# Chunk products added to the context by an accumulating DMA, in a two-layer graph-attention kernel

## The chip, the cores and the metric

The kernel runs on one core of one Trainium2 chip. A core has five engines that run side by side and wait for each other through semaphores: TensorE (PE in the profile, with its weight loads as PEld), VectorE (DVE), ScalarE (ACT), GpSimd (POOL) and SyncE (SP), which here issues all DMAs. The metric is the device time of one launch in microseconds (us), lower is better; of several runs the median is taken.

## The reference

Eight batches of 2048 nodes with 256 features go through two layers. Layer 0 is attention with 4 heads of width 64, in which the keys are cut into 8 chunks of 256 and each chunk has a softmax of its own; the chunk outputs are added up. Layer 1 is a graph attention whose scores are sums of one term per row and one per column. All is in float32.

```python
# layer 0
q, k, v = x @ Wq.T + bq, x @ Wk.T + bk, x @ Wv.T + bv        # 4 heads of 64
scores = einsum('bhnd,bhjcd->bhnjc', q, kc) / sqrt(64)       # j: 8 chunks, c: 256 keys
scores = where(mask == 0, -10, clip(scores, -10, 10))
attn = softmax(scores, axis=-1)                              # within each chunk
ctx = einsum('bhnjc,bhjcd->bhnd', attn, vc)                  # sums over the chunks j
h = layernorm(x + layernorm_affine(ctx @ Wo.T + bo + x))
# layer 1
Wh = h @ W
e = leaky_relu((Wh @ a1)[:, :, None] + (Wh @ a2)[:, None, :])
attention = softmax(where(adj > 0 or i == j, e, -inf))
out = layernorm(h + elu(attention @ Wh))
```

## The kernel before

Work of layer 0 is a loop `J` over 8 batches x 4 query blocks of 512 rows x 8 chunks. A query block is called a quarter here (quarter 0 to 3 of a batch). A chunk has two halves of 128 keys, and each half is one beat, or half-step: in a beat PE makes the scores of one half chunk for four heads (L689), DVE clips and masks them in PSUM (L699), ACT takes their exponential into `e` (L702). In the two beats after a chunk is complete, PE makes its products: the sums of `e` (part 2, with a matrix of ones) and the two halves of `e` times `v` (parts 0 and 1), all at L715. ACT copies the sums to `ds` (L729) and the products to `un` (L723). From `ds` a small DMA, a reciprocal on DVE (L737) and two more DMAs through HBM make `r`, one over the sum, spread over all rows of a head. Two beats later `scaled` (L745 to L753) runs: DVE multiplies `un` by `r`, into the context `ctxT` for the first chunk (L748), in place for the others (L750), and GpSimd adds the result to `ctxT` (L751), 7 times a block and 224 times in all. `ctxT` has one buffer for a block, `un` and `ds` have two.

The last addition of a block is issued at the end of one beat; the output projection `po` of that block (L331, 16 matmuls on PE, in the generator `fin`) stands at the end of the beat after. `fin` also loads x, adds the biases on GpSimd (L322, L323), makes two layer norms and stores h to HBM (`h_d`) and its transpose.

Layer 1 runs beside layer 0, behind it by somewhat more than a batch, at 1.5 of its steps per beat. One step treats 128 columns of a block of 512 rows: ACT (L524) and DVE (L528) make the leaky relu, DVE masks it (L533), ACT takes the exponential (L537), GpSimd adds it to the row sums `acc` (L546), PE multiplies with Wh (L556, in the last batch L571). A prelude per batch finds row maxima on DVE (L432). When a block of 16 steps is done, its tail `fin1` (L469 to L492) runs one piece per beat: the load of h into `hr`; division by the sum and the exponential `ex` of elu (L484); the minimum and maximum on DVE (L486) with the addition of `hr` on GpSimd (L487); the statistics of the layer norm (`st_c`, L292 to L295); normalization and the store. `hx`, `hr` and `ex` have one buffer each.

The order of the instructions on each engine is the order in which this program issues them (the schedule is written out by hand): at the end of a beat come the layer-1 products, then the pieces of the preludes, then of `fin` and `fin1` in the order in which they were begun, then the agenda, which holds `inverse`, `spread` and `scaled`. Each engine takes its instructions strictly in that order, and so does SP's queue of DMAs.

The lines that the change touches are L226, L469 to L492, L708, L728 and L751.

Of the kernel before, what the change touches and what calls it, by code (L numbers as in the profile page):

```python
# [9 lines left out]
F32 = mybir.dt.float32  # L10
# [4 lines left out]
ALU = mybir.AluOpType  # L15
# [4 lines left out]
P = 128  # L20
# [8 lines left out]
def tile_adj_attention__then__gat(  # L29
# [35 lines left out]
    nc = tc.nc  # L65
    B, N, F = x.shape
# [4 lines left out]
    IB = 512  # L71
# [151 lines left out]
    nc.sync.dma_start(out=W_aug[:, :, 0:F], in_=W.rearrange("(k p) o -> p k o", p=P))  # L223
    a_bc = []
    for n in range(2):
        t = one.tile([P, F], F32, tag=("hx", "ex")[n], name=f"a_bc{n}")  # L226
        nc.sync.dma_start(out=t, in_=a[n * F : (n + 1) * F, :].rearrange("f o -> (f o)").partition_broadcast(P))
        a_bc.append(t)

# [238 lines left out]

    def fin1(b, ib, hx, acc):  # L469

        hr = one.tile([P, TPB, F], F32, tag="hr", name=f"hr{b}_{ib}")
        nc.sync.dma_start(out=hr, in_=h_d[b, ib])
        yield


        if acc is not None:
            pr = ps_m.tile([P, TPB], F32, tag="m", name=f"pr{b}_{ib}")
            for t in range(TPB):
                nc.tensor.matmul(pr[:, t : t + 1], acc[:, ts(t, P)], ones[:, 0:1], start=True, stop=True)
            r = two.tile([P, TPB], F32, tag="r1", name=f"r1{b}_{ib}")  # L480
            nc.vector.reciprocal(r, pr)
            divided(hx, [hx[:, t, :] for t in range(TPB)], r)
        ex = one.tile([P, TPB, F], F32, tag="ex", name=f"ex{b}_{ib}")
        nc.scalar.activation(ex, hx, AF.Exp, bias=shifts[:, 2:3])  # L484
        yield
        nc.vector.scalar_tensor_tensor(hx, ex, 1.0, hx, ALU.min, ALU.max)  # L486
        nc.gpsimd.tensor_add(hx, hx, hr)  # L487
        yield
        mv, rstd = stats(hx, f"c{b}_{ib}")
        yield  # L490
        normalize(hx, mv, rstd, f"c{b}_{ib}")
        nc.sync.dma_start(out=out[b, ts(ib, IB), :].rearrange("(t p) f -> p t f", p=P), in_=hx)  # L492
# [170 lines left out]
    for J in range(total + 1):  # L663
        b, ib, j = J // (NIB * NCH), J // NCH % NIB, J % NCH
        live = J < total
        if live and j == 0:
            ctxT = one.tile([P, 2, IB], F32, tag="ctx", name=f"ctxT{b}_{ib}")
        cur = {"b": b, "ib": ib, "j": j, "es": [], "ctxT": ctxT, "v": None, "name": f"{b}_{ib}_{j}"}
        for half in range(2):
            c = 2 * j + half  # L670
            if live:

                if c % HT == 0:
                    if b == 0:
                        mk = blocks0[ib, c // HT]
                    else:
                        mk = mk0.pop((b, ib, c // HT))
                if c % HT == 1:
                    n = (b * NIB + ib) * 2 + c // HT + 1
                    nb, nib, nhf = n // (2 * NIB), n // 2 % NIB, n % 2  # L680
                    if 0 < nb < B:
                        mk0[nb, nib, nhf] = mask_block(0, nib, nhf, f"{nb}_{nib}_{nhf}")
            begin_beat(RATE if b < B - 1 else LAST_RATE)
            if live:
                scs = []
                for hp in range(NPAIR):
                    sc = ps_s.tile([P, 2, IB], F32, tag="sc", name=f"sc{b}_{ib}_{c}_{hp}")
                    for h in range(2):
                        nc.tensor.matmul(  # L689
                            sc[:, h, :],  # L690
                            kT[h * D : (h + 1) * D, hp, ts(c, P)],
                            qT[h * D : (h + 1) * D, hp, :],
                            start=True,
                            stop=True,
                        )
                    scs.append(sc)
                cap = mk[:, c % HT, :].unsqueeze(1).to_broadcast([P, 2, IB])
                for hp in range(NPAIR):
                    nc.vector.scalar_tensor_tensor(scs[hp], scs[hp], -CLIP, cap, ALU.max, ALU.min)  # L699
                for hp in range(NPAIR):  # L700
                    e = eight.tile([P, 2, IB], F32, tag="e", name=f"e{b}_{ib}_{c}_{hp}")
                    nc.scalar.activation(e, scs[hp], AF.Exp)  # L702
                    cur["es"].append(e)
            middle_of_beat()

            if prev is not None:
                if half == 0:
                    prev["un"] = two.tile([P, 2, IB], F32, tag="un", name=f"un{prev['name']}")  # L708
                for part in ((2, 0), (1,))[half]:
                    m = ps_m.tile([P, IB], F32, tag="m", name=f"u{prev['name']}_{part}")  # L710
                    for i in range(2):
                        pc = 2 * prev["j"] + i
                        for h in range(H):
                            f0 = h * D + part * DH
                            nc.tensor.matmul(  # L715
                                m[h * DH : (h + 1) * DH, :],
                                prev["v"][:, pc, f0 : f0 + DH] if part < 2 else ones[:, 0:DH],
                                prev["es"][2 * i + h // 2][:, h % 2, :],
                                start=(i == 0),
                                stop=(i == 1),  # L720
                            )
                    if part < 2:
                        nc.scalar.copy(prev["un"][:, part, :], m)  # L723
                    else:

                        ds = two.tile([P, IB], F32, tag="ds", name=f"ds{prev['name']}")  # L728
                        nc.scalar.copy(ds, m)  # L729
                        dc = two.tile([P, IB // DH], F32, tag="dc", name=f"dc{prev['name']}")  # L730
                        nc.sync.dma_start(
                            out=dc, in_=ds.rearrange("(h m) (n w) -> h m n w", m=DH, n=DH)[:, 0, :, :]
                        )
                        prev["dc"] = dc

                        def inverse(p=prev):
                            nc.vector.reciprocal(p["dc"], p["dc"])  # L737
                            p["rd"] = dram3.tile([H, IB], F32, tag="rd", name=f"rd{p['name']}")
                            nc.sync.dma_start(out=p["rd"].rearrange("h (m w) -> (h m) w", m=DH), in_=p["dc"])

                        def spread(p=prev):
                            p["r"] = two.tile([P, IB], F32, tag="r", name=f"r{p['name']}")
                            nc.sync.dma_start(out=p["r"], in_=p["rd"].unsqueeze(1).to_broadcast([H, DH, IB]))

                        def scaled(p=prev):  # L745
                            r2 = p["r"].unsqueeze(1).to_broadcast([P, 2, IB])
                            if p["j"] == 0:
                                nc.vector.tensor_mul(p["ctxT"], p["un"], r2)  # L748
                            else:
                                nc.vector.tensor_mul(p["un"], p["un"], r2)  # L750
                                nc.gpsimd.tensor_add(p["ctxT"], p["ctxT"], p["un"])  # L751
                            if p["j"] == NCH - 3:
                                fins.append(fin(p["b"], p["ib"], p["ctxT"]))  # L753

                        at(beat, inverse)
                        at(beat, spread)
                        at(beat + 2, scaled)

            end_beat()
            if half == 1:  # L760


                if live and j == NCH - 2 and J + 2 < total:
                    nb, nib = (b, ib + 1) if ib + 1 < NIB else (b + 1, 0)
                    xq = xT_tile(nb, nib, "q")
                    if nb != b:
                        tiles = [xT_tile(nb, i, "k") for i in range(2)]
                if live and j == NCH - 1 and J + 1 < total:
                    qT = make_qT(nb, nib, xq)
                    if nb != b:  # L770
                        kT = make_kT(nb, tiles)
                        tiles_v = [xT_tile(nb, i, "v") for i in range(3)]
                if live and J % (NIB * NCH) == 0:
                    if b == 0:
                        tiles_v = [xT_tile(0, i, "v") for i in range(3)]
                    v = make_v(b, tiles_v)
                if live:
                    cur["v"] = v
            beat += 1
        prev = cur if live else None  # L780
# [50 lines left out]
```

## Time and profile before

| | us |
|---|---|
| median of 3 runs | 4443.78 |
| lowest and highest | 4443.62, 4454.05 |
| the profiled execution, reported time | 4445.93 |
| its span, first to last instruction | 4444.1 |
| span without both layers side by side: first 600 us, last 644.1 us | 1244.1 |

The mean granted clock of TensorE was 0.976. The profile names a group of instructions by line, engine, operation and the tiles it writes and reads (`out<-in`). A wait "A <- B" is idle time of A's engine that ended when B finished. The chain of waits follows the work back from the last instruction. Tile names have their buffer numbers left out.

These are the DMAs that the changed lines are concerned with, from the page (issuing queue, count, size):

```profile
r<-rd SPq DMA_DIRECT2D x256, 256.0 KB
fb<-far SPq DMA_DIRECT2D x256, 256.0 KB
```

### The profile page before, as it was taken

To read this page: it belongs to the slowest core of one execution; us is meant where nothing else is said; L and a number is where in the kernel's file an instruction comes from. 1 tells how busy PE (TensorE), PEld (TensorE's weight loads), DVE (VectorE), ACT (ScalarE), POOL (GpSimd) and SP (SyncE) were. 2 spreads that over 40 slices of the span, in tenths; PEclk is the share of its full clock that TensorE was granted. 3 is DMA by queue.
4 is the path that set the end of the run, shared out by engine and by line. 5 is a ranking of instruction groups with operands and counts; after the bars stand their busy time and mean duration, and the time that the engine had idled before them with its cause. 6 is when DMAs were issued, how large, how long until landed. Compare 5 with 4: busy or idle time off the path is not lost. (4 is left out here: it accounts for less than half of the span.)

```text
span 4444.1 us, 61341 instructions
## 1 busy us (share of the span) xinstructions
PE 4076.1 (92%) x23052; PEld 1914.3 (43%) x23052; DVE 3405.3 (77%) x4527; ACT 2603.7 (59%) x3877; POOL 1776.4 (40%) x906
## 2 busy tenths in 40 slices
PE   7888999999899998999999999999989999899767
PEld 3222334444344543445334453444434444344545
DVE  4777469985799758996599866998579975898686
ACT  4665445665556655665556655666555665566445
POOL 0222224553355423554345542455325553355411
PEclk9999999999999999999999999999999999999988
DMA  4554333332322323323333223332232232332241
GB/s 149 167 164 152 92 100 101 96 93 78 105 81 91 101 64 115 89 77 92 99 99 91 78 77 104 101 101 86 84 101 87 86 103 68 118 92 73 65 136 54
DMA packets 266874, 433.98 MB, mean 98 GB/s; under 512 B 86097, under 2 KB 121169, under 8 KB 265553
## 3 DMA queue, kind: packets, MB, share of 16 engines
q1 hardware_dynamic: 266576, 430.06, 31.7%
q8 instruction: 181, 2.97, 0.3%
q14 instruction: 117, 0.95, 0.1%
HBM read 358.48 MB, written 69.40 MB: 96 GB/s over the span
## 5 line engine op out<-in xcount | busy, mean ns | idle before, releaser
L702 ACT ACTIVATE e<-sc 128x1024 f32<-128x1024 f32 x1024 | 1037.3, 1022 | 1146.7 <-DVE sc L699 1102.2
L699 DVE SCALAR_TENSOR_TENSOR sc<-sc,mk 128x1024 f32<-128x1024 f32 x1024 | 1205.8, 1222 | 512.8 <-PE sc L689 282.9
L689 PE MATMUL sc<-qT,kT 64*128 64x512 f32 x4096 | 1060.0, 632 | 106.9 <-ACT e L702 104.0
L751 POOL TENSOR_TENSOR ctxT<-ctxT,un 128x1024 f32<-128x1024 f32 x224 | 562.7, 2512 | 1164.1 <-DVE un L750 1059.1
L715 PE MATMUL u<-e,v 128*32 128x512 f32 x8192 | 980.4, 596 | 0.0
L556 PE MATMUL us<-wh,w 128*128 128x256 f32 x3584 | 875.5, 393 | 78.1 <-ACT w L537 60.5
L556 PEld LDWEIGHTS us<-wh,w 128*128 128x128 f32 x3584 | 662.8, 192 | 420.7 <-ACT w L537 117.7
L546 POOL TENSOR_TENSOR acc<-acc,w 128x512 f32<-128x512 f32 x392 | 602.7, 1537 | 541.0 <-ACT w L537 531.3
L689 PEld LDWEIGHTS sc<-qT,kT 64*128 64x128 f32 x4096 | 346.1, 188 | 627.4 <-ACT e L702 307.4
L528 DVE SCALAR_TENSOR_TENSOR w<-ab,sj,w 128x512 f32<-128x512 f32 x512 | 584.0, 1161 | 32.1 <-ACT w L524 32.1
L715 PEld LDWEIGHTS u<-e,v 128*32 128x32 f32 x8192 | 239.8, 110 | 657.7 <-issue 539.2
L533 DVE TENSOR_TENSOR w<-w,mk 128x512 f32<-128x512 f32 x512 | 475.1, 948 | 44.4 <-DMA mk<-mask 41.7
L715 PE MATMUL u<-e,ones 128*32 128x512 f32 x4096 | 498.3, 604 | 0.0
L432 DVE CUSTOM_DVE_ANT_0 fb<-sj_row,fb 128x1024 bf16<-128x1024 f32 x256 | 397.1, 1559 | 5.9 <-DMA fb<-far 5.6
L537 ACT ACTIVATE w<-w 128x512 f32<-128x512 f32 x512 | 310.7, 631 | 90.0 <-DVE w L533 89.6
L524 ACT ACTIVATE w<-ab,sj 128x512 f32<-128x512 f32 x512 | 353.3, 716 | 13.5 <-PE us L571 6.3
L750 DVE TENSOR_TENSOR un<-un,r 128x1024 f32<-128x1024 f32 x224 | 276.5, 1234 | 85.4 <-DMA r<-rd 78.8
L723 ACT COPY un<-u 128x512 f32<-128x512 f32 x512 | 300.6, 587 | 55.4 <-PE u L715 53.7
L715 PEld LDWEIGHTS u<-e,ones 128*32 128x32 f32 x4096 | 107.9, 110 | 359.5 <-issue 317.9
L737 DVE RECIPROCAL dc<-dc 128x16 f32<-128x16 f32 x256 | 64.1, 250 | 184.5 <-DMA dc<-ds 159.7
L571 PE MATMUL us<-wh,w 128*128 128x257 f32 x512 | 128.7, 413 | 45.9 <-ACT w L537 45.7
L487 POOL TENSOR_TENSOR hx<-hx,hr 128x1024 f32<-128x1024 f32 x32 | 91.6, 2862 | 191.6 <-DVE hx L486 191.6
(97 smaller groups left out, 3150.7 us busy)
## 6 DMA issues: line engine op xcount, KB each, us to landing
r<-rd SPq DMA_DIRECT2D x256, 256.0 KB
fb<-far SPq DMA_DIRECT2D x256, 256.0 KB
mk<-mask SPq DMA_DIRECT2D x120, 512.0 KB
xT_k<-in_xT_dram SPq DMA_DIRECT2D x32, 512.0 KB
raw<-in_adjT_dram SPq DMA_DIRECT2D x32, 512.0 KB
xT_q<-in_xT_dram SPq DMA_DIRECT2D x32, 512.0 KB
rawf<-in_adj_dram SPq DMA_DIRECT2D x32, 512.0 KB
xT_v<-in_xT_dram SPq DMA_DIRECT2D x32, 512.0 KB
```

The costliest lines, as they stand in the source:

```text
L432: nc.vector.tensor_tensor_reduce(out=fbs[2 * TPB * ib + n], in0=sj_row[:, ts(n % 2, HN)], in1=fbs[2 * TPB * ib + n], scale=1.0, scalar=2 * ...
L524: nc.scalar.activation(self.w, k["ab"][:, 1, :], AF.Identity, bias=k["sj"][:, 1, c : c + 1])
L528: nc.vector.scalar_tensor_tensor(self.w, k["ab"][:, 0, :], k["sj"][:, 0, c : c + 1], self.w, ALU.add, ALU.max)
L533: nc.vector.tensor_tensor(self.w, self.w, self.k["mks"][self.c // HT][:, self.c % HT, :], ALU.min)
L537: nc.scalar.activation(self.w, self.w, AF.Exp)
L546: nc.gpsimd.tensor_add(k["acc"], k["acc"], self.w)
L556: nc.tensor.matmul(k["us"][:, t, :], self.w[:, ts(t, P)], k["wh"][:, c, 0:F], start=(first and t % 2 == 0), stop=last, skip_group_check=True,)
L689: nc.tensor.matmul(sc[:, h, :], kT[h * D : (h + 1) * D, hp, ts(c, P)], qT[h * D : (h + 1) * D, hp, :], start=True, stop=True,)
L699: nc.vector.scalar_tensor_tensor(scs[hp], scs[hp], -CLIP, cap, ALU.max, ALU.min)
L702: nc.scalar.activation(e, scs[hp], AF.Exp)
L715: nc.tensor.matmul(m[h * DH : (h + 1) * DH, :], prev["v"][:, pc, f0 : f0 + DH] if part < 2 else ones[:, 0:DH], prev["es"][2 * i + h // 2][ ...
L751: nc.gpsimd.tensor_add(p["ctxT"], p["ctxT"], p["un"])
```

## The change

The product of a chunk is added to `ctxT` by a DMA from SBUF to SBUF with an add on its way, issued from GpSimd's queue, in place of GpSimd's own addition. `un` gets three buffers and `ds` one. `ex` shares the buffer of `hr` (so that h is loaded only after the minimum and maximum have read `ex`), and the addition of h moves to the beat after. A vector that is loaded once at the start, and lay in the buffer of `ex`, lies in that of `y`.

```diff
@@ a_bc @@
-        t = one.tile([P, F], F32, tag=("hx", "ex")[n], name=f"a_bc{n}")
+        t = one.tile([P, F], F32, tag=("hx", "y")[n], name=f"a_bc{n}")
@@ fin1 @@
-        hr = one.tile([P, TPB, F], F32, tag="hr", name=f"hr{b}_{ib}")
-        nc.sync.dma_start(out=hr, in_=h_d[b, ib])
         yield
...
-        ex = one.tile([P, TPB, F], F32, tag="ex", name=f"ex{b}_{ib}")
+        ex = one.tile([P, TPB, F], F32, tag="hr", name=f"ex{b}_{ib}")
         nc.scalar.activation(ex, hx, AF.Exp, bias=shifts[:, 2:3])
         yield
         nc.vector.scalar_tensor_tensor(hx, ex, 1.0, hx, ALU.min, ALU.max)
+        hr = one.tile([P, TPB, F], F32, tag="hr", name=f"hr{b}_{ib}")
+        nc.sync.dma_start(out=hr, in_=h_d[b, ib])
+        yield
         nc.gpsimd.tensor_add(hx, hx, hr)
@@ the loop over chunks @@
-                    prev["un"] = two.tile([P, 2, IB], F32, tag="un", name=f"un{prev['name']}")
+                    prev["un"] = three.tile([P, 2, IB], F32, tag="un", name=f"un{prev['name']}")
...
-                        ds = two.tile([P, IB], F32, tag="ds", name=f"ds{prev['name']}")
+                        ds = one.tile([P, IB], F32, tag="ds", name=f"ds{prev['name']}")
...
                                 nc.vector.tensor_mul(p["un"], p["un"], r2)
-                                nc.gpsimd.tensor_add(p["ctxT"], p["ctxT"], p["un"])
+                                nc.gpsimd.dma_start(out=p["ctxT"], in_=p["un"], accum_op=ALU.add)
```

## The prediction

> **What bounds the kernel now.** I read the page's first part, then busy time by stage, then the waits on TensorE, and last the timeline around single accumulations. The first line is from the page, the second from the busy times by window (columns: stretch, its length, busy us of each engine, granted clock, DMA share, GB/s).
>
> ```profile
> PE 4076.1 (92%) x23052; PEld 1914.3 (43%) x23052; DVE 3405.3 (77%) x4527; ACT 2603.7 (59%) x3877; POOL 1776.4 (40%) x906
> 600.00:3800.00 3200.00, 3044.77 (x17479) 1429.25 (x17467) 2534.46 (x3279) 1914.12 (x2881) 1417.20 (x724) 0.99 0.30 92
> ```
>
> In the 3200 us in which both layers run, PE is busy 3044.8 us, 95%. Its matmuls stand; only its 155 us of gaps there (368 us in the whole span) can shrink, and a new gap on PE is a loss almost in full. The waits view says what ends those gaps (total us, times, longest us):
>
> ```profile
> PE sc L689 <- ACT e L702: 104.0, 68, 6.6
> PE us L556 <- ACT w L537: 60.5, 49, 6.8
> PE po L331 <- POOL ctxT L751: 26.8, 16, 5.1
> ```
>
> The third is the line under change: the output projection `po` waits for the last accumulation of its block. That is 16 of 32 blocks already, so this edge has no cushion there. The add itself, and the VectorE rows that could feel it, in the groups (count | busy, mean ns | idle before):
>
> ```profile
> L751 POOL TENSOR_TENSOR ctxT<-ctxT,un 128x1024 f32<-128x1024 f32 x224 | 562.7, 2512 | 1164.1 <-DVE un L750 1059.1
> L528 DVE SCALAR_TENSOR_TENSOR w<-ab,sj,w 128x512 f32<-128x512 f32 x512 | 584.0, 1161 | 32.1 <-ACT w L524 32.1
> ```
>
> 224 adds take 562.7 us on an engine that is 40% busy, so its time as such bounds nothing. L528, whose fastest run is 649 ns and median 746, averages 1161. The timeline shows why, in one block of query quarter 3:
>
> ```profile
> 2626.64 1.22 DVE L750 TENSOR_TENSOR un<-un,r 128x1024 f32<-128x1024 f32 x1
> 2627.94 2.36 POOL L751 TENSOR_TENSOR ctxT<-ctxT,un 128x1024 f32<-128x1024 f32 x1 [3.39 <-DVE un L750]
> 2629.11 1.74 DVE L528 SCALAR_TENSOR_TENSOR w<-ab,sj,w 128x512 f32<-128x512 f32 x1
> 2636.66 3.62 PE L331 MATMUL po<-WT_o,ctxT 128*128 128x256 f32 x16
> ```
>
> L528 started beside the add and ended with it (1.74 us). Here PE came to `po` 8.80 us after L750's end (2636.66 less 2627.86), so a slow landing costs nothing. Quarter 2 is different:
>
> ```profile
> 1949.08 1.23 DVE L750 TENSOR_TENSOR un<-un,r 128x1024 f32<-128x1024 f32 x1
> 1951.16 2.34 POOL L751 TENSOR_TENSOR ctxT<-ctxT,un 128x1024 f32<-128x1024 f32 x1
> 1953.55 3.72 PE L331 MATMUL po<-WT_o,ctxT 128*128 128x256 f32 x16 [1.32 <-POOL ctxT L751]
> ```
>
> PE was free 1.93 us after L750's end and then stood still for 1.32 us.
>
> **What the Trainium skill says.** (1) "SBUF — State Buffer", Who interferes with whom: a VectorE instruction with two SBUF inputs contends with a GpSimd instruction that reads SBUF, and the second to start waits for the first. The trace agrees: over all 512 L528s, the 101 that overlap most with L751 average 1501 ns, the 180 beside no GpSimd work 736. L699, which has PSUM for one input, is 1220 ns beside L751 and 1223 alone. (2) "DMA: Bandwidth & Descriptors", Anatomy of one DMA: a DMA from GpSimd takes about 2.0 us plus bytes/436e3. No run here has such a DMA. (3) The same page, Rules for kernel authors: an accumulate reads its destination and writes it later, so a reader must wait for its semaphore; `po` then waits for landing, not for the issue. (4) "Perfetto Trace Analysis", DMA Instruction — SWDGE: the instruction's end in a profile is the end of descriptor generation, not of the movement; the POOL row will thus look short.
>
> **The change part by part.** The sum is against the profiled execution: span 4444.1, reported 4445.9 us, 2.1 above the median of 4443.8.
>
> *Landing instead of add.* Let X be the time from L750's end until `ctxT` may be read. It is now 2.4 to 3.2 us (2.49 when the add starts at once). For 512 KB formula (2) gives 3.2; the destination has to be read as well, so I count the bytes twice: an estimate of 2.0 + 2.4 = 4.4. In this trace an HBM load of the same 512 KB took 3.63 us from issue to release when quiet (chain of waits, `mk<-mask` at 4301.92) and 7.52 when crowded (at 3846.74). Behind every accumulation SP issues the 256 KB `r<-rd` within 2 us, so some crowding is regular. I take X = 5.5; bounds 4.4 and 10. From the timeline I took, for each of the 32 blocks, when PE was free for `po` after L750's end. Quarter 0: 2.58 us early to 2.3 late, mostly near 0 or 2; quarter 1: 0.0 once, else 4.7 to 5.3; quarter 2: 1.93 in six, about 0 and 3.6 in the others; quarter 3: 4.1 to 8.8. The sum of max(0, X minus that) is 53 us at 4.4, 76 at 5.5, 89 at 6, 142 at 8, 202 at 10, against today's 26.8. At 5.5: **+50 us**.
>
> *The other accumulations.* They follow each other at a median of 15.3 us, so each lands before the next; the GpSimd queue does not stall. With three `un` buffers ACT's copy L723 meets a buffer whose DMA was issued four half-steps (some 35 us) earlier, and the one `ds` buffer is refilled about 17 us after its 8 KB DMA, which takes about 2 us. All of these: 0. If X passed 15 us, POOL's sums of `w` and its layer-norm steps behind the wait would be late.
>
> *h one step later.* Instruction order on PE is the same; on DVE, ACT, POOL and SP the tail of a layer-1 block (add of h, statistics, normalization, store) moves one half-step back. In six quarter-2 blocks its statistics (nine instructions, 2.3 us, 1946.75 to 1949.1) now stand directly before L750; they go behind it, so L750 ends 2.3 us earlier against PE: 6 x 2.3 = **-14**. They then stand in the half-step with `po` and push L699 there; half of 2.3 us in six blocks reaches PE: **+7** (0 to 14). SP's h load now waits for L486 (DVE); behind it in SP's queue are `rd<-dc` and `r<-rd`, which wait for a later DVE instruction anyway, so 0. At the very end nothing covers the load. From the chain of waits (start, us, what):
>
> ```profile
> 4430.51 1.24 DVE hx L486
> 4431.86 2.34 POOL hx L487
> ```
>
> L487 follows L486 at once; a 512 KB load comes between, at the quiet 3.63: **+3.6**. The tag swap of `ex` and `a_bc` is free: nothing else holds these buffers then.
>
> *The shared port.* Without L751, 101 L528s lose about 0.77 us each and 15 L432s about 0.75 (1966 beside it, 1214 alone): 89 us of DVE. DVE is not the bound, and PE's gaps behind it (first two waits, 165 us, of which about 66 in the 3200 us) mostly follow other GpSimd adds (L322, L323). I give a quarter: **-22** (0 to -60). POOL's own 563 us shrink to descriptor writing: 0.
>
> Sum: 50 - 14 + 7 + 3.6 - 22 = +25, so 4445.9 + 24.6 = 4470.5 for such an execution, and 4468 for the median.
>
> **Rivals.** *Faster: the port decides.* Removing L751 frees VectorE not only directly; L432 and L528 pairs move up, GpSimd's remaining adds meet other instructions, and PE's 104 us of waiting for `e` melt. For it: 89 us of measured lengthening. Against it: PE is 95% busy. With X at its lower end and the port at -40: 26 - 14 + 0 + 4 - 40 = -24, 4420. It decides as soon as the port gives more than the new waiting on `po`: with X = 4.4 from 16 to 23 us of relief, with 5.5 from about 47.
> *The landing is long.* Accumulation works at less than half the copy rate, or its queue shares the engines badly; X = 8 to 10. At 8: 115 - 14 + 14 + 4 - 10 = +109, 4553; at 10 about 4610. Against it: DMA engines are only 30% busy.
> *Nothing to measure.* Relief and waiting cancel, 4440 to 4455: X near 4.8.
>
> **Chances.** Forecast (slower by up to 90 us) 0.45; long landing 0.17; faster 0.27; cancelled 0.11. About 0.3%, 13 us, is what a measurement of this kernel can tell from no change; a little of the forecast's own case falls inside it, so: faster 0.27, same 0.14, slower 0.59. The range 4420 to 4555 goes from the faster rival's worked value to the long landing at 8 us; the forecast's own is 4445 to 4515.
>
> **What would show it.** PE's wait of `po` on the DMA of `ctxT` grows from 26.8 to about 60 us, in quarters 0 and 2 most, hardly in 3; L528's mean falls from 1161 towards 1010; in the last block L487 starts some 3.6 us later after L486. I am wrong if `po` waits less than 30 us in all (X was too long), if it waits over 100 (too short), or if PE's waits for `e` and `w` fall by more than 40 us (the port was worth more).

## The result and the profile after

The change makes the kernel slower: 4597.26 us (median of 4 runs, 4590.40 to 4600.67) against 4447.48 (4 runs, 4443.62 to 4454.05); ratio 1.0343, 95% interval 1.0328 to 1.0357. That is about 150 us. The profiled execution took 4590.4 us with a span of 4588.6 (before: 4444.1); TensorE's mean granted clock was 0.958 (before 0.976). In the changed kernel the lines up to the start of `fin1` keep their numbers and most later ones move by one: `un` times `r` is L751, the DMA is L752, the scores are L690, the exponential is L703, the addition of `hr` is L488.

From the page of the changed kernel, its busy times and its new DMA queue (packets, MB, share of the 16 engines' time):

```profile
PE 4120.5 (90%) x23052; PEld 1942.2 (42%) x23052; DVE 3267.5 (71%) x4527; ACT 2610.0 (57%) x3877; POOL 1312.1 (29%) x906
q0 software_dynamic: 32256, 117.45, 13.9%
```

The same 23052 matmuls keep PE busy 44.4 us longer (4120.5 against 4076.1), and it idles 100.1 us longer (4588.6 - 4120.5 = 468.1 against 368.0). The traces also record the clock that PE is granted: PE's busy time at half of it rose from 161.7 to 262.1 us, and half of that difference, 50.2 us, is about as much as the busy time grew. GpSimd and VectorE have less to do, as meant. The accumulations hold the DMA engines for 13.9% of the span, beside SP's own 31%.

What ends PE's gaps, from the waits view of the changed kernel (total us, times, longest):

```profile
PE sc L690 <- ACT e L703: 130.6, 77, 8.4
PE po L331 <- DMA ctxT<-un: 90.2, 18, 9.4
```

Before, the first was 104.0 and the wait of `po` 26.8. The tile view of `ctxT` in the changed kernel gives the time from issue to landing of all 224 accumulations:

```profile
DMA to landing us min/median/max: 4.5/5.1/9.5
```

Counted from L751's end, the last one of a block landed after 4.8 to 6.2 us. So X, the time from L751's end until `ctxT` may be read, was as forecast. The waiting wasn't: with these landings and the slacks of before it would be 70 us in place of 90.2. PE no longer comes to `po` when it did. VectorE's waits for loads, before:

```profile
DVE un L750 <- DMA r<-rd: 78.8, 25, 7.5
DVE w L533 <- DMA mk<-mask: 41.7, 14, 4.7
DVE fb L432 <- DMA fb<-far: 5.6, 5, 3.8
```

and after:

```profile
DVE un L751 <- DMA r<-rd: 154.5, 52, 8.1
DVE w L534 <- DMA mk<-mask: 63.8, 15, 6.4
DVE fb L432 <- DMA fb<-far: 24.2, 16, 3.4
```

Three loads on SP's queue, none of which the change touches, arrive late more often: 242.5 us of waiting against 126.1. The timeline of the changed kernel shows what that does to a quarter-0 block:

```profile
2842.90 1.23 DVE L432 CUSTOM_DVE_ANT_0 fb<-sj_row,fb 128x1024 bf16<-128x1024 f32 x1 [1.33 <-DMA fb<-far]
...
2844.05 1.22 DVE L751 TENSOR_TENSOR un<-un,r 128x1024 f32<-128x1024 f32 x1
...
2845.57 0.86 POOL L752 DMA_DIRECT2D ctxT<-un  x1 [7.70 <-DVE dc L738]
...
2850.56 5.38 PE L331 MATMUL po<-WT_o,ctxT 128*128 128x256 f32 x16 [4.67 <-DMA ctxT<-un]
```

VectorE stood 1.33 us for `fb`, and L751, which is next in its order, came that much later. PE was free 0.62 us after L751's end (2850.56 - 4.67 - 2845.27); in the same block before it was 2.32. Then it stood for 4.67 us, and the 16 matmuls after the stall took 5.38 us; the same 16 took 3.72 before.

The loss begins early. Busy times by window (stretch, length, busy us of PE, PEld, DVE, ACT, POOL, clock, DMA share, GB/s), before and then after:

```profile
0.00:600.00 600.00, 507.49 (x2864) 184.15 (x2868) 355.30 (x499) 335.88 (x434) 129.01 (x62) 0.95 0.46 141
```

```profile
0.00:600.00 600.00, 475.65 (x2612) 170.12 (x2616) 334.72 (x481) 313.30 (x396) 78.05 (x59) 0.91 0.57 158
```

In its first 600 us PE got through 252 matmuls fewer. At the projection of block 4 (the second batch) the changed kernel is 51 us behind, then 9 to 21 us more for each batch (131 at block 28), and 13.5 more in the last stretch.

### The profile page after: what moved, and what is told of

It is laid out like the page before. It is cut to its first block, busy times and chain, and to the rows that moved or that the text cites. A ratio compares the mean times of both kernels' runs of the same rounds, so it can differ in the third digit from the quotient of the medians.

```text
span 4588.6 us, 61639 instructions
## 1 busy us (share of the span) xinstructions
PE 4120.5 (90%) x23052; PEld 1942.2 (42%) x23052; DVE 3267.5 (71%) x4527; ACT 2610.0 (57%) x3877; POOL 1312.1 (29%) x906
## 3 DMA queue, kind: packets, MB, share of 16 engines
q0 software_dynamic: 32256, 117.45, 13.9%
## 5 line engine op out<-in xcount | busy, mean ns | idle before, releaser
L703 ACT ACTIVATE e<-sc 128x1024 f32<-128x1024 f32 x1024 | 1038.1, 1022 | 1277.7 <-DVE sc L700 1232.1
L690 PE MATMUL sc<-qT,kT 64*128 64x512 f32 x4096 | 1076.7, 640 | 132.7 <-ACT e L703 130.6
L547 POOL TENSOR_TENSOR acc<-acc,w 128x512 f32<-128x512 f32 x392 | 558.7, 1425 | 701.2 <-ACT w L538 679.7
L690 PEld LDWEIGHTS sc<-qT,kT 64*128 64x128 f32 x4096 | 354.3, 191 | 657.8 <-ACT e L703 311.5
L752 POOL DMA_DIRECT2D ctxT<-un x224 | 196.7, 878 | 1381.3 <-DVE un L751 646.2
L534 DVE TENSOR_TENSOR w<-w,mk 128x512 f32<-128x512 f32 x512 | 516.6, 1029 | 66.6 <-DMA mk<-mask 63.8
L529 DVE SCALAR_TENSOR_TENSOR w<-ab,sj,w 128x512 f32<-128x512 f32 x512 | 464.4, 927 | 34.8 <-ACT w L525 34.7
L751 DVE TENSOR_TENSOR un<-un,r 128x1024 f32<-128x1024 f32 x224 | 292.1, 1304 | 161.7 <-DMA r<-rd 154.5
L432 DVE CUSTOM_DVE_ANT_0 fb<-sj_row,fb 128x1024 bf16<-128x1024 f32 x256 | 359.5, 1411 | 24.5 <-DMA fb<-far 24.2
L331 PE MATMUL po<-WT_o,ctxT 128*128 128x256 f32 x512 | 144.9, 446 | 92.4 <-DMA ctxT<-un 90.2
L738 DVE RECIPROCAL dc<-dc 128x16 f32<-128x16 f32 x256 | 63.8, 249 | 192.3 <-DMA dc<-ds 165.6
```

What stands on the lines that cost most here:

```text
L432: nc.vector.tensor_tensor_reduce(out=fbs[2 * TPB * ib + n], in0=sj_row[:, ts(n % 2, HN)], in1=fbs[2 * TPB * ib + n], scale=1.0, scalar=2 * ...
L529: nc.vector.scalar_tensor_tensor(self.w, k["ab"][:, 0, :], k["sj"][:, 0, c : c + 1], self.w, ALU.add, ALU.max)
L534: nc.vector.tensor_tensor(self.w, self.w, self.k["mks"][self.c // HT][:, self.c % HT, :], ALU.min)
L547: nc.gpsimd.tensor_add(k["acc"], k["acc"], self.w)
L690: nc.tensor.matmul(sc[:, h, :], kT[h * D : (h + 1) * D, hp, ts(c, P)], qT[h * D : (h + 1) * D, hp, :], start=True, stop=True,)
```

## Experiments

All ratios are to the kernel before, timed beside each of them on the same chip; per cents below are of about 4440 us.

### The parts alone

**fin1_only**: the changed `fin1`, GpSimd's addition kept, `un` and `ds` with two buffers.

```diff
-                                nc.gpsimd.dma_start(out=p["ctxT"], in_=p["un"], accum_op=ALU.add)
+                                nc.gpsimd.tensor_add(p["ctxT"], p["ctxT"], p["un"])
```

> The kernel before with only the second half of the change: ex in the buffer of hr, h loaded after the minimum and maximum and added a beat later; GpSimd still adds the products. Three theories. Edge: the loss of 150 us comes from the output projection waiting for the landing of the last accumulation, and from the slower clock after each such stall; then this kernel stays within 0.5% of before, 4430 to 4465 us. Move: the later h pushes the multiplication of un behind in quarter 0; then at least 40 us slower, 4485 or more. Traffic: the 224 transfers delay the other DMAs; then as with edge, no change here.

Measured: 4453.94 us, ratio 1.0035 (1.0022 to 1.0048): +15 us.

**dma_only**: the kernel before with the accumulating DMA and nothing else (two `un` buffers, `fin1` as it was).

```diff
-                                nc.gpsimd.tensor_add(p["ctxT"], p["ctxT"], p["un"])
+                                nc.gpsimd.dma_start(out=p["ctxT"], in_=p["un"], accum_op=ALU.add)
```

> The kernel before with only the addition replaced by the accumulating DMA; un and ds keep two buffers, fin1 is as before. Edge and traffic: about as slow as the changed kernel, 4560 to 4610 us, with the wait of po on the DMA at 80 us or more. Move: at most half of the loss, 4520 or less, since the multiplication of un in quarter 0 then stands where it stood.

Measured: 4596.02 us, ratio 1.0353 (1.0333 to 1.0373), the whole loss. The third `un` buffer and the moved addition change nothing that can be seen beside it, though the moved addition alone cost 15 us; the DMA is the cause.

### The last accumulation against the six before it

**only_last_dma**: the kernel before, and of the seven additions of a block only the last one, for which `po` waits, is a DMA (32 of 224).

```diff
-                                nc.gpsimd.tensor_add(p["ctxT"], p["ctxT"], p["un"])
+                                if p["j"] == NCH - 1:
+                                    nc.gpsimd.dma_start(out=p["ctxT"], in_=p["un"], accum_op=ALU.add)
+                                else:
+                                    nc.gpsimd.tensor_add(p["ctxT"], p["ctxT"], p["un"])
```

> The kernel before, in which only the last of the seven additions of a block (32 of 224) is an accumulating DMA. Edge: nearly the whole loss, 4555 us or more, and po waits 80 us or more. Traffic: 32 of 224 transfers bring a seventh of the loss beside the bare landing, so 4500 or less, and po waits some 60 us, the sum of the slacks of before at a landing of 5.2 us less the 27 that it waited already, plus those.

Measured: 4513.91 us, ratio 1.0167 (1.0151 to 1.0184): +74 us, between the two. A line of its page:

```profile
PE 4100.0 (91%) x23052; PEld 1929.8 (43%) x23052; DVE 3392.3 (75%) x4527; ACT 2604.4 (58%) x3877; POOL 1728.2 (38%) x906
```

and one of its waits view:

```profile
PE po L331 <- DMA ctxT<-un: 78.2, 20, 8.7
```

The wait of `po` grew by 51.4 us (78.2 less 26.8), which is the +50 of the prediction. But PE was also busy 23.9 us longer with the same matmuls (4100.0 against 4076.1): what a stall costs is not only its length.

**last_by_add**: the reverse, the changed kernel with GpSimd's addition for the last chunk (192 DMAs).

```diff
-                                nc.gpsimd.dma_start(out=p["ctxT"], in_=p["un"], accum_op=ALU.add)
+                                if p["j"] < NCH - 1:
+                                    nc.gpsimd.dma_start(out=p["ctxT"], in_=p["un"], accum_op=ALU.add)
+                                else:
+                                    nc.gpsimd.tensor_add(p["ctxT"], p["ctxT"], p["un"])
```

> The changed kernel, in which the last addition of each block is made by GpSimd again; the other six stay accumulating DMAs (192 of 224). Edge: back to the time before or slightly under it, 4420 to 4460 us, since the port is still freed in six of seven chunks. Traffic: most of the loss stays, above 4520, and the first batch stays 40 us or more behind.

Measured: 4530.74 us, ratio 1.0204 (1.0189 to 1.0219). The six early accumulations, for which nothing on PE waits, cost more than the last one: 90 us here, although GpSimd is spared six of seven additions.

**drop_six**: the kernel before without six of the seven additions: the context lacks six chunks. It frees the shared port and GpSimd, which is busy 516.5 us less, and adds no transfer.

```diff
-                                nc.gpsimd.tensor_add(p["ctxT"], p["ctxT"], p["un"])
+                                if p["j"] == NCH - 1:
+                                    nc.gpsimd.tensor_add(p["ctxT"], p["ctxT"], p["un"])
```

> The kernel before without six of the seven additions of a block: only the last product is added, by GpSimd, so the context lacks six chunks. It prices the freed port alone. As predicted, a quarter of the 89 us of lengthened VectorE work reaches the time: 4405 to 4425 us. Rival: the port is worth its full bound, 4375 to 4390; or nothing, 4432 to 4442.

Measured: 4409.31 us, ratio 0.9934 (0.9919 to 0.9948). The two together are worth 0.66%, 29 us; they are called the freed port below. With that the six transfers cost 2.04 - 0.35 (the changed `fin1`) + 0.66 = 2.35%, about 104 us, with an uncertainty of some 11 us from the three intervals. This takes the 0.35% as there in last_by_add too; if the moved addition costs nothing beside the DMAs, as dma_only suggests, it is 2.70%, 120 us.

**not_first_batch**: GpSimd adds in the first batch, the DMA in the other seven.

```diff
-                                nc.gpsimd.dma_start(out=p["ctxT"], in_=p["un"], accum_op=ALU.add)
+                                if p["b"] > 0:
+                                    nc.gpsimd.dma_start(out=p["ctxT"], in_=p["un"], accum_op=ALU.add)
+                                else:
+                                    nc.gpsimd.tensor_add(p["ctxT"], p["ctxT"], p["un"])
```

> The changed kernel with GpSimd's addition in the first batch (28 of 224) and the DMA in the other seven. The changed kernel falls 51 us behind by the fifth block. Traffic (in the first batch the DMA engines are busiest): 45 to 55 us come back, 4540 to 4555 us. Rival: each transfer costs alike, so 28 of 224 are an eighth, 20 us, 4575 to 4580.

Measured: 4539.88 us, ratio 1.0227 (1.0211 to 1.0242): 1.16%, 51 us less than the changed kernel, for 28 of 224 DMAs. The loss is largest where the DMA engines had most to do already (46% busy before in the first 600 us, 30% in the middle). It isn't all due to the early transfers: `po` waits 71.0 us in this run (61.0 for the DMA, 10.0 for GpSimd), 19 less than in the changed kernel. Nor does the run tell the busy DMA engines from another thing that sets the first batch apart: layer 1, whose work could fill PE's gaps, doesn't run there yet.

### Attempts that failed

**po_later**: the changed kernel with `po` one beat later, so that the landing is covered.

```diff
@@ fin, ahead of po @@
+        yield
```

> The changed kernel with the output projection and all that follows it in its generator one beat later. Edge: the 90 us of waiting for the landing and the slow clock after it go, 4485 to 4530 us, traffic stays. Rival, if landing is not what po waits for: 4580 or more.

Measured: 4787.57 us, ratio 1.0792 (1.0774 to 1.0810). Two lines of its waits view:

```profile
DVE dc L739 <- DMA dc<-ds: 326.5, 165, 6.1
PE sc L691 <- ACT e L704: 323.3, 106, 10.3
```

`po` now waits 1.8 us in all for the DMA, but the first of these waits has doubled and the second is two and a half times as long (165.6 and 130.6 in the changed kernel). A likely reason, which wasn't tested, is that the projection and its VectorE part fell into the beat in which `dc` is needed. A later `po` alone costs more than it covers, so the run says nothing of the price of the landing.

**acc_beside**: fin1_only, and beside each addition an accumulating DMA of `un` into a tile that nobody reads.

```diff
+    beside = const.tile([P, 2, IB], F32, name="beside")
+    nc.vector.memset(beside, 0.0)
...
                                 nc.gpsimd.tensor_add(p["ctxT"], p["ctxT"], p["un"])
+                                nc.gpsimd.dma_start(out=beside, in_=p["un"], accum_op=ALU.add)
```

> The kernel with only the second half of the change (h a beat later, 4454 us) and GpSimd's additions kept; beside each of the 224 additions un is also sent by an accumulating DMA into a spare tile that nothing reads, so the result is the same and nobody but the next refill of un waits for the transfer. Traffic: the load on the DMA engines costs by itself what the six early transfers of a block cost, 90 to 110 us, so 4530 to 4570, and un waits for r about 150 us instead of 79. Rival, waits: transfers that nobody waits for cost nothing, the loss with six transfers a block is in the order of the queues; then 4445 to 4475.

Measured: 4614.41 us, ratio 1.0398 (1.0380 to 1.0416), slower than the changed kernel itself. Its waits view names a wait that only this kernel has:

```profile
ACT un L726 <- DMA beside<-un: 94.7, 39, 6.9
```

With two `un` buffers ACT's copy meets a DMA that still reads its buffer. The run mixes traffic with a new buffer wait; the next one has three buffers.

**acc_beside_3**: the same with three `un` buffers, one `ds`, and 384 of 512 columns (room for the tile).

```diff
-                                nc.gpsimd.dma_start(out=beside, in_=p["un"], accum_op=ALU.add)
+                                nc.gpsimd.dma_start(out=beside, in_=p["un"][:, :, 0:384], accum_op=ALU.add)
```

> The changed kernel, three buffers of un, with GpSimd's additions back, and beside each addition an accumulating DMA of three quarters of un into a spare tile that nothing reads. With three buffers ACT's refill of un should not wait for it (in acc_beside it waited 95 us). Traffic alone: three quarters of about 124 us (the 94 us of the six early transfers in last_by_add and the 30 us of the freed port in drop_six, which this kernel does not get), so 4530 to 4565. Rival: acc_beside was slow from the refill of un; then 4450 to 4480.

Measured: 4578.55 us, ratio 1.0317 (1.0301 to 1.0332): 2.82%, 125 us over fin1_only, somewhat more than expected.

**late_issue**: last_by_add with its six early DMAs issued one beat later, away from the beat in which SP sends `rd` and `r`.

```diff
+                        def sent(p=prev):
+                            if 0 < p["j"] < NCH - 1:
+                                nc.gpsimd.dma_start(out=p["ctxT"], in_=p["un"], accum_op=ALU.add)
...
+                        at(beat + 3, sent)
```

> As last_by_add (4531 us), with the six accumulating DMAs of a block issued one beat later, so that they no longer start beside the load of r that SP issues in the same beat. Collision: the loss of the six comes from r arriving late at VectorE; then un waits for r 70 to 100 us instead of 151, and the time is 4440 to 4490 us. Load: any 512 KB read-modify-write hurts wherever it lies; then 4515 to 4545.

Measured: 4569.06 us, ratio 1.0298 (1.0278 to 1.0317), 0.94% slower than last_by_add. From its waits view:

```profile
DVE dc L738 <- DMA dc<-ds: 194.9, 122, 5.2
DVE un L751 <- DMA r<-rd: 157.5, 51, 8.5
```

`r` is as late as before (151.4 us in last_by_add), and now the small `dc<-ds` is late too. So it was no clash with `r` alone that an offset of one beat would undo. Other offsets weren't tried.

**warm_po**: the changed kernel with 24 matmuls on the weights ahead of `po` in the blocks with the longest waits, to keep PE busy through the stall.

```diff
+            if t2 == 0 and (ib == 0 or b == 0 and ib < 3):
+                for _ in range(24):
+                    nc.tensor.matmul(po[:, 0, :], WT["o"][:, 0, 0:P], WT["o"][:, 0, :], start=True, stop=True)
```

> The changed kernel with 24 matmuls on weights, their result overwritten by the projection, ahead of po in the 11 blocks in which po waits longest (quarter 0 of each batch, quarters 1 and 2 of the first): some 5.6 us of work that fits in the wait of 7 to 9 us. Clock: TensorE runs at half its clock for some us after such a stall, so keeping it busy gains 1.7 to 3.4 us a block, 4560 to 4580 us. Rival, the stall costs only its length: 4590 to 4605.

Measured: 4593.33 us, ratio 1.0350 (1.0334 to 1.0365), no difference from the changed kernel. Two groups of its page (the added matmuls stand at L331, `po` at L334):

```profile
L334 PE MATMUL po<-WT_o,ctxT 128*128 128x256 f32 x512 | 116.6, 380 | 13.4 <-DMA ctxT<-un 11.2 <-ACT un L727 2.2
L331 PE MATMUL po<-WT_o 128*128 128x256 f32 x480 | 106.3, 381 | 0.0
```

The mean matmul of `po` fell from 446 ns to 380, and PE's busy time without the added ones from 4120.5 to 4093.8. But the condition holds in ten blocks, and in each the added ones run for 10.6 us (106.3 / 10), longer than any of the stalls they fill (4.7 to 9.4 us in the changed kernel). PE idles 77.6 us less than in the changed kernel and is busy 79.6 us longer: `po` began later by about what it then gained. A filling of fitting length wasn't tried.

### What it is in the transfers

**small_beside**: acc_beside_3 with 48 columns instead of 384.

```diff
-                                nc.gpsimd.dma_start(out=beside, in_=p["un"][:, :, 0:384], accum_op=ALU.add)
+                                nc.gpsimd.dma_start(out=beside[:, :, 0:48], in_=p["un"][:, :, 0:48], accum_op=ALU.add)
```

> acc_beside_3 with the same 224 accumulating DMAs into the tile that nobody reads, but 48 instead of 384 columns of each half of un: the same number of issues on GpSimd and of rows, an eighth of the bytes. Reference points: fin1_only 4454 us (no such DMA), acc_beside_3 4579. If the bytes on the DMA engines cost the 125 us, an eighth of them costs some 15 to 40 and the time is 4465 to 4495. If the number of issues or rows costs it (GpSimd's 0.9 us for each issue in its order, or the writing of the rows' descriptors), it stays at 4550 to 4585.

**copy_beside**: acc_beside_3 with a plain copy.

```diff
-                                nc.gpsimd.dma_start(out=beside, in_=p["un"][:, :, 0:384], accum_op=ALU.add)
+                                nc.gpsimd.dma_start(out=beside, in_=p["un"][:, :, 0:384])
```

> acc_beside_3 with a plain copy in place of the accumulation: the same 224 issues and the same bytes of un, into the same unread tile, but the destination isn't read first. If it is the accumulation that makes these transfers dear[...], a copy costs some half: 4500 to 4530 us. If any transfer of this size costs the same, whatever it does at the destination, the time stays at 4560 to 4590.

Measured: small_beside 4511.96 us, ratio 1.0174 (1.0158 to 1.0189); copy_beside 4488.23 us, ratio 1.0122 (1.0106 to 1.0139). Both miss their expectations: small_beside falls between the two, copy_beside below both. The tile views of the added DMA tell why, first small_beside, then copy_beside (duration of the issue on GpSimd in ns, min/median/max):

```profile
L755 POOL DMA_DIRECT2D beside<-un x224: 1159/1187/1611, 96.0 to 4212.4; - x112
```

```profile
L755 POOL DMA_DIRECT2D beside<-un x224: 722/722/902, 94.4 to 4182.4; - x112
```

The issues come on top of GpSimd's additions, 267 us of its time in one and 164 in the other, and stand ahead of its other work. That is a cost which the changed kernel doesn't have. acc_beside_3 has it too (1202 ns an issue), and small_beside, with the same issues and an eighth of the bytes, still lost 62 us against fin1_only; so half of acc_beside_3's 125 us may not be traffic. So the question was put again in the changed kernel's own order, without the additions:

**small_six**: last_by_add, its six DMAs cut to 128 of 1024 columns. **copy_six**: last_by_add, its six DMAs as plain copies over the context.

```diff
-                                    nc.gpsimd.dma_start(out=p["ctxT"], in_=p["un"], accum_op=ALU.add)
+                                    nc.gpsimd.dma_start(out=p["ctxT"][:, 0:1, 0:128], in_=p["un"][:, 0:1, 0:128], accum_op=ALU.add)
```

```diff
-                                    nc.gpsimd.dma_start(out=p["ctxT"], in_=p["un"], accum_op=ALU.add)
+                                    nc.gpsimd.dma_start(out=p["ctxT"], in_=p["un"])
```

> last_by_add with its six early accumulating DMAs cut to 128 of 1024 columns of un (the same 192 issues and the same 128 rows each, 64 KB instead of 512 KB; the context lacks the rest of six chunks). Between drop_six (4409 us, no such DMA) and last_by_add (4531). The beside runs had GpSimd's adds and its DMA issues one after the other, so that GpSimd's time was part of their loss; here the adds are gone. If the bytes on the DMA engines cost the 122 us, an eighth of them leaves 4415 to 4435. If the number of issues costs it (GpSimd's 0.9 us, the ordering of the accumulations one behind the other), it stays at 4500 to 4535.

> last_by_add with its six early DMAs as plain copies of un over the context instead of accumulations (same 192 issues, same 512 KB; the context holds only the last two chunks). From the beside runs a copy takes half the DMA engines' time for the same bytes (5.9% against 11.8%): if that time is what costs, half of the 122 us is left and the time is 4455 to 4485. If bytes moved cost it whatever their kind, it stays at 4515 to 4535; if only the accumulation costs, it falls to 4410 to 4430.

Measured: small_six 4421.87 us, ratio 0.9965 (0.9954 to 0.9977); copy_six 4461.75 us, ratio 1.0053 (1.0038 to 1.0068). The shares of the DMA engines' time, from the DMA views of small_six, copy_six and last_by_add:

```profile
q0 software_dynamic: 27648, 12.60, 2.5%
```

```profile
q0 software_dynamic: 27648, 100.68, 5.8%
```

```profile
q0 software_dynamic: 27648, 100.68, 12.1%
```

All three have the same number of packets. Less the changed `fin1` (0.35%) and with the freed port (0.66%) put back, the six transfers cost nothing in small_six (-0.35 - 0.35 + 0.66 = -0.04%), 0.84% or 37 us in copy_six, and 104 us in last_by_add. (Without the 0.35% these are 0.31%, 1.19% and 2.70%; the differences between the three runs, which all have the changed `fin1` and the same additions, don't depend on it: 39 us from small_six to copy_six, 106 to last_by_add.) So it isn't their number, and not the bytes of `un` as such: the cost rises with the time for which they hold the DMA engines, and an accumulation holds them twice as long as a copy of the same bytes. VectorE's waits for loads follow, from the waits views in the same order:

```profile
DVE un L751 <- DMA r<-rd: 72.9, 26, 5.7
DVE w L534 <- DMA mk<-mask: 38.6, 15, 4.5
DVE fb L432 <- DMA fb<-far: 11.0, 10, 3.7
```

```profile
DVE un L751 <- DMA r<-rd: 103.1, 36, 7.5
DVE w L534 <- DMA mk<-mask: 44.2, 15, 5.4
DVE fb L432 <- DMA fb<-far: 18.5, 13, 3.7
```

```profile
DVE un L751 <- DMA r<-rd: 151.4, 52, 6.3
DVE w L534 <- DMA mk<-mask: 61.8, 15, 6.0
DVE fb L432 <- DMA fb<-far: 22.7, 16, 3.9
```

Their sums are 122.5, 165.8 and 235.9 us. The loads themselves come later: of the times that `r` was waited for, the longest from SP's issue to the multiplication's start was 6.8 us, 8.6 and 10.3. Two other explanations find no support in these traces: VectorE's own work hardly lengthens (busy 3257.8, 3250.8 and 3279.0 us), and GpSimd, which is busy for less than a third of the span, waits little for accumulations to land (27.5 us in last_by_add). What comes out on PE, in the waits views of small_six and last_by_add:

```profile
PE sc L690 <- ACT e L703: 92.4, 68, 6.4
...
PE po L331 <- POOL ctxT L755: 28.0, 10, 5.4
```

```profile
PE sc L690 <- ACT e L703: 133.9, 82, 8.0
...
PE po L331 <- POOL ctxT L755: 46.2, 12, 6.0
```

A late load holds VectorE, which takes its instructions in order; behind it are the clipping of the scores, and so `e`, and L751. These views show the two ends of this chain growing together; the links between weren't followed one by one. From small_six to last_by_add the span grows by 110.9 us (4418.7 to 4529.6): PE idles 75.8 us longer (41.5 on `e`, 18.2 on `po`, 9.2 on a load of its own, `xT_q`), and is busy 35.1 us longer (4070.9 to 4106.0). Its busy time at half the clock rises from 165.0 to 231.9 us, so 33.5 of these 35.1 are the clock.

No version that computes the whole context beat the kernel before. drop_six puts the ceiling for getting rid of six of the seven additions at 29 us.

## Why the prediction was right in sign and wrong in size

It forecast 4468 us with a range up to 4555; the changed kernel takes 4597.

- **The other accumulations, "All of these: 0": this step failed.** They cost 104 us (last_by_add, fin1_only and drop_six). Each does land before the next, as argued, and GpSimd's queue hardly stalls. Left out was what they do to others. The prediction wrote that SP issues `r<-rd` within 2 us behind every accumulation (in the trace before, it does so behind about half of the additions, 108 of 222), and used that only to lengthen X; for `r`, `fb` and the masks, which share the DMA engines with it, it counted nothing. The Trainium skill has the point ("DMA: Bandwidth & Descriptors", Issuing engines are not separate DMA queues: DMAs of whichever engine run on the same 16 and interleave), and the runs agree: VectorE's three waits, 126.1 us before, are 242.5. "DMA engines are only 30% busy" stood in the text as an argument against trouble; it is a mean over a long stretch, and where the loads of the first batch run it was 46% before and 57% after.
- **Landing, +50: right in kind, short in size.** X was 4.8 to 6.2 us for 5.5 taken. Alone, in only_last_dma, it added 51.4 us of waiting. It cost 74 us all the same: PE was busy 23.9 us longer, and the prediction had no term for that. In the changed kernel `po` waits 90.2 us, 63.4 more, since the slack was read from the timeline before: in quarter 0 PE there came to `po` from 2.58 us too early to 2.3 late, and now in seven of eight blocks 1.5 to 3.1 too early. PE's mean slack in quarter 0 is 0.8 us late before, 0.5 early in small_six, 1.4 in copy_six, 1.9 in last_by_add and in the changed kernel: half of the shift has come in small_six already, the rest grows with the load.
- **The shared port, -22: near in size, by a guess.** drop_six gives -29. But VectorE's busy time fell there by 130.5 us (3405.3 to 3274.8), where 89 were counted, and GpSimd's own freed time, put at 0, is in the same -29; the quarter had no measurement behind it. In the changed kernel L528 (now L529) has a mean of 927 ns, from 1161; 1010 was forecast:

```profile
L529 DVE SCALAR_TENSOR_TENSOR w<-ab,sj,w 128x512 f32<-128x512 f32 x512 | 464.4, 927 | 34.8 <-ACT w L525 34.7
```

  In drop_six it is 1046, in small_six, which has the later h, 926; so the later h has a share in the fall.

- **h one step later, -14 + 7 + 3.6: wrong, +15.** In fin1_only the wait of `po` did fall, from 26.8 to 16.5 us, and in quarter 2 PE's slack rose from 1.93 us to nearly 4. The end costs more: in its profile fin1_only is 2.3 us ahead at the last projection and 6.8 behind at the end. The chain of the changed kernel shows the load at work there:

```profile
4571.47 1.24 DVE hx L484
4572.72 3.45 DMA hr<-h_d
4576.32 2.34 POOL hx L488
```

3.45 us between L484 and L488 is the step as forecast (3.6), but the chain runs through this load in all four blocks of the last batch, not once, and one of the four takes 6.95 us (7.52 in fin1_only). So the end costs 9 us in the profile of fin1_only where 3.6 were forecast. The rest of the 15 us wasn't traced.

The parts add up: +15 - 29 + 104 + 74 = +164 against 152. As the 104 was worked out with the 15 and the 29, this shows no more than that last_by_add (+90) and only_last_dma (+74) together make about the whole. Of the rivals, the long landing came nearest in time, but not by its X of 8 to 10 us: X was 4.8 to 6.2. Its remark that the queue may share the engines badly pointed the right way, and was counted in X alone. The signs named to show the forecast wrong (`po` below 30 or over 100 us, `e` and `w` falling by 40) would have let this one through; a sign for the loads on SP's queue was missing.

## What to carry to other kernels

A DMA that nobody waits for is not free: multiply its engine time by its count, and look in the waits view for loads that arrive just in time, for those pay. Count an accumulation as twice a copy. When slack is taken from the timeline before, ask first whether the change itself shifts the instruction that the slack is counted from.

## What the runs showed of the hardware

- **The price of an accumulating DMA.** 512 KB from SBUF to SBUF landed 3.1 us (median) after issue as a copy (copy_six) and 5.1 us as an accumulation (last_by_add). The first agrees with the 3.2 that the formula of the Trainium skill ("DMA: Bandwidth & Descriptors", Anatomy of one DMA) gives; the second is above the 4.4 that was estimated by counting the bytes twice. 64 KB accumulated landed after 2.4 us (small_six). In a busier place the formula doesn't hold: the 384 KB copy of copy_beside landed after 5.1 us (median), where it gives 2.9.
- **A stall on PE can be paid twice.** After 4.67 us of waiting (block 20) `po` took 5.38 us instead of 3.72, and after 7.02 us (block 4) 5.53 instead of 3.72. The clock record of the traces shows what happens: the granted clock is 1 or 0.5, and 0.5 in stretches that are nearly all 3.413 us or a multiple of it. The Trainium skill ("TensorE: Matmul & The Clock Gate", Part 1: The HAM clock gate) states that after an idle window of about 3.4 us PE runs at half its clock until it has been busy for about as long. The stretches agree with that; as for the stall that it takes, shorter ones sufficed here too. In eight traces (before, after, fin1_only, drop_six, only_last_dma, last_by_add, small_six, copy_six) all 55 projections that had waited over 2.6 us took over 4.1 us, of the 29 that had waited 1.5 to 2.6 us 16 did (11 of them with the clock at 0.5), and of the other 172 only 5. Of the 144.5 us by which the span of the changed kernel grew, 44.4 are longer busy time of PE: 18.7 in `po` (126.2 to 144.9), 16.7 in the scores (1060.0 to 1076.7), which wait for `e`.
